# A graph network on one core: TensorE transposes for the first graph's input and for the tiles of the last five graphs

## The chip, the core and the metric

One Trainium2 core runs the whole program: 64 graphs, one after the other through the same layers. The time is the device time of one execution in microseconds, the median of three runs. The core has a matrix engine (TensorE, PE in the profile), a vector engine (VectorE, DVE), an activation engine (ScalarE, ACT), GpSimd (POOL) and a queue that issues transfers (SyncE, SP). They run side by side and wait for one another through semaphores; each takes its own instructions in the order in which the program lists them.

## What is computed

Every graph has 256 nodes with 256 features (float32) and an adjacency matrix of 256 x 256 integers. Four layers follow one another, each with a residual and a layer norm:

```python
x: (64, 256, 256)   adj: (64, 256, 256)
# layer 0: attention over 8 heads of 32 under the mask adj | adj.T | eye, then a feed-forward of 1024
qkv = x @ Wqkv.T + bqkv
x = norm(x + norm(norm(x + softmax(mask(q k^T / sqrt(32))) v @ Wo.T + bo) + relu(. @ W1.T + b1) @ W2.T + b2))
# layers 1 and 2: graph attention ("gat")
h = x @ W;  e = leaky_relu(f_i + g_j) under the mask;  x = norm(x + softmax(e) @ h [+ bias, or elu])
# layer 3: two relational convolutions ("conv"), rel is adj == 1
h = elu(x @ w_root + b + (rel^T @ x / deg) @ w_rel)   # twice
x = norm(x + h)
```

TensorE contracts over the partition axis, of which there are 128. A product `x @ W` therefore needs x with the features on the partitions, that is, transposed. Each graph needs this six times: for the input of the attention, for the feed-forward, for the two gats and for the two convs.

## The kernel before

The kernel first writes down all operations of all graphs with an engine, an assumed cost, and the tiles that they read and write. A list scheduler then sorts them by due times; what it puts out is the fixed order of instructions on each engine. The due times of the last five graphs lie close together (`LAST, SPACE = 5, 0.1`), so that these graphs run interleaved at the end.

```python
RINGS = {"x": 3, "adj": 4, ..., "T": 4, ..., "blocks": 1, "turned": 1, "xT": 2}   # buffers of each kind
LAG = {"PE": 0.21, "DVE": 0.13, "ACT": 0.13, "POOL": 0.08, "SP": 4.5}
PERIOD = 46.0
LAST, SPACE = 5, 0.1
```

There are three ways of transposing. The first is that of the feed-forward: four TensorE transposes into one PSUM bank, and a copy by ScalarE.

```python
def transposed(xt):
    xT, pt = new("T", [P, KB, N]), new("bank", [P, KB, N])
    def issue():
        for kb in range(KB):
            for i in range(NB):
                nc.tensor.transpose(pt()[:, kb, i * P : (i + 1) * P], xt()[:, i, kb * P : (kb + 1) * P], ident)
    pe("full", 0.44, issue, [xt], [pt], [xT])
    act(0.47, lambda: nc.scalar.copy(xT(), pt()), [pt], [xT])
    return xT
```

The second, the "bounce", serves the gats and the convs. VectorE transposes each 32 x 32 block within the tile; four transfers write the blocks to device memory in the right places, and one reads the whole back. The rows come back in another order of the features (feature 32 b + c at partition 4 c + b), so the weights of these layers are loaded in that order too (`spread` in the setup).

```python
def bounced(xt):
    turned, rows, xT = new("turned", ...), new("rows", ...), new("T", [P, NB * KB, P])
    dve(0.63, lambda: nc.vector.transpose(turned().rearrange("p b q n -> p (b q n)"),
                                          xt().rearrange("p i (k c b) -> p b (i k) c", k=KB, b=4)), [xt], [turned], "uses")
    for a in range(4):
        op("SP", 0.5, lambda a=a: nc.sync.dma_start(rows()..., turned()[32 * a : 32 * a + 32]...), ...)
    op("SP", 0.5, lambda: nc.sync.dma_start(xT()..., rows()...), [rows], [xT], lag=BACK)
    return xT, lambda kb, i: xT()[:, KB * i + kb, :]
```

The third serves the input. Eight loads bring the blocks of x to their places straight from the input, 32 floats at a time, and VectorE transposes the blocks.

```python
def input_transposed():
    blocks, xT = new("blocks", [P, KB, N // 32, 32]), new("xT", [P, KB, N])
    for a in range(4):
        for kb in range(KB):
            f = kb * P + 32 * a
            op("SP", 0.51, lambda ...: nc.sync.dma_start(blocks()[32 * a : 32 * a + 32, kb],
               x_in[g, :, f : f + 32].rearrange("(m r) c -> r m c", r=32)), [], [(blocks, 4 * kb + a)])
    dve(0.62, lambda: nc.vector.transpose(xT()..., blocks()...), [blocks], [xT], "uses")
    return xT
```

The setup and one graph, cut:

```python
def setup():
    load(c_wqkv, wqkv, "WqkvT")          # one transfer of 768 KB
    load(c_wo, wo, "WoT"); load(c_w1, w1, "W1T"); load(c_w2, w2, "W2T")
    ...                                  # gat and conv weights

def projections(xT):                     # q and k in halves, then v
    ...  pe("full", 0.86, product(wqkv[:, kb, n * P : (n + 1) * P], xT...), [xT, c_wqkv], [pq], [qk])
    ...  pe("full", 0.86, product(xT..., wqkv[:, kb, 2 * D : 3 * D]),       [xT, c_wqkv], [pv], [v])

# one graph
xT = input_transposed()
adj = load("adj", adj_graph[g], I32)
am, gm = masks(adj)
xt = load("x", x_graph[g], F32)
add_row_later(xt, bo, [c_bo])
ctxT = attention(xT, am)
x1 = product_plus(...); layer_norm(x1)
xt = feed_forward(x1, load("xr", x_graph[g], F32))
xt = layer1(xt, gm)                      # gat: begins with bounced(xt)
xt = layer2(xt, gm)                      # gat
rel = relation(load("adj", adj_graph[g], I32))
h = conv(conv(xt, 0, rel, rdeg), 1, rel, rdeg)   # each begins with bounced(.)
add(h, xt); layer_norm(h)
op("SP", 0.4, lambda: nc.sync.dma_start(out_graph[g], h()), [h], [])
```

Of the kernel before, what the change touches and what calls it, by code (L numbers as in the profile page):

```python
# [8 lines left out]
F32 = mybir.dt.float32  # L9
# [8 lines left out]
P = 128  # L18
# [2 lines left out]
BIG = 1e30  # L21
NO_EDGE = -346.0


SENT, BACK = 3.0, 4.5

# [186 lines left out]
def tile_gnn_stack(ctx: ExitStack, tc: tile.TileContext, t: dict, out: bass.AP):  # L213
# [16 lines left out]
    nc = tc.nc  # L230
    x_in, adj_in = t["x"], t["adj"]
    B, N, D = x_in.shape
# [253 lines left out]
    def main_path(plan):  # L486
# [19 lines left out]
        def setup():  # L506


            def load(w, to, name, rel=None):
                view = t[name] if rel is None else t[name][rel]  # L510
                n = view.shape[0] * view.shape[1] / (256 * 256)
                plan.op("SP", 0.85 * n, lambda: nc.sync.dma_start(to, view.rearrange("(c p) n -> p c n", p=P)), 0, [], [w])

            def spread(w, to, name, rel=None):

                view = (t[name] if rel is None else t[name][rel]).rearrange("(k b c) n -> b c k n", b=4, c=32)
                for b in range(4):
                    plan.op("SP", 0.6, lambda b=b: nc.sync.dma_start(to[b::4], view[b]), 0, [], [w])

            load(c_wqkv, wqkv, "WqkvT")  # L520
            load(c_wo, wo, "WoT")
            load(c_w1, w1, "W1T")
            load(c_w2, w2, "W2T")
            for i, names in enumerate((("L1_WT", "L1_W"), ("L2_W", "L2_WT"))):

                wt = plan.tile("T", [P, KB, D], F32)
                plan.op("SP", 0.85, lambda wt=wt, n=names[1]: nc.sync.dma_start(wt(), t[n].rearrange("(c p) n -> p c n", p=P)),
                        0, [], [wt])
                spread(c_gw[i], gw[i][:, :, 0:D], names[0])
                for kb in range(KB):  # L530
                    pa = plan.tile("bank", [P, 2], F32)

                    def issue(i=i, kb=kb, wt=wt, pa=pa):
                        for c in range(KB):
                            nc.tensor.matmul(pa(), lhsT=wt()[:, c, kb * P : (kb + 1) * P], rhs=av[i][:, :, c],
                                             start=(c == 0), stop=(c == KB - 1))

                    plan.op("PE", 0.9, issue, 0, [wt], [pa], mode="full")
                    plan.op("DVE", 0.2, lambda i=i, kb=kb, pa=pa: nc.vector.tensor_copy(ga[i][:, kb, :], pa()),
                            0, [pa], [c_ga[i]])  # L540
                for b in range(4):
                    plan.op("SP", 0.6, lambda i=i, b=b: nc.sync.dma_start(gw[i][b::4, :, D : D + 2], ga[i][32 * b : 32 * b + 32]),
                            0, [c_ga[i]], [c_gw[i]])
            for i in range(2):
                spread(c_cw[i], conv_w[i][:, :, 0:D], f"w_root{i + 1}")
                spread(c_cw[i], conv_w[i][:, :, D:], f"w_rel{i + 1}", 1)


            pb = plan.tile("bank", [P, D], F32)

            def bias_out():
                for c in range(KB):
                    nc.tensor.matmul(pb(), lhsT=bqkv[:, 2 * KB + c : 2 * KB + c + 1].to_broadcast([P, P]), rhs=wo[:, c, :],
                                     start=(c == 0), stop=(c == KB - 1))

            plan.op("PE", 0.9, bias_out, 0, [c_wo], [pb], mode="full")
            plan.op("DVE", 0.34, lambda: nc.vector.tensor_tensor(bo, pb(), bo, op=ALU.add), 0, [pb], [c_bo])


            pf = plan.tile("bank", [P, NF], F32)  # L560
            for f in range(NF):
                def shift(f=f):
                    for c in range(KB):
                        nc.tensor.matmul(pf()[:, f : f + 1], lhsT=w1[:, c, f * P : (f + 1) * P], rhs=bcol[:, c : c + 1],
                                         start=(c == 0), stop=(c == KB - 1))

                plan.op("PE", 0.9, shift, 0, [c_w1], [pf], mode="full")
            plan.op("DVE", 0.2, lambda: nc.vector.tensor_tensor(b1, pf(), b1, op=ALU.add), 0, [pf], [c_b1])
            for c in range(KB):
                plan.op("DVE", 0.7, lambda c=c: nc.vector.tensor_scalar(w1[:, c, :], w1[:, c, :], gcol[:, c : c + 1], None,  # L570
                                                                        op0=ALU.mult), 0, [c_w1], [c_w1])

        def graph(g):
# [9 lines left out]
            def act(cost, issue, reads, writes):  # L583
                op("ACT", cost, issue, reads, writes)
# [4 lines left out]
            def tok(ring, dtype=F32):  # L589
                return new(ring, [P, NB, D], dtype)  # L590

            def load(ring, view, dtype):
                xt = tok(ring, dtype)
                op("SP", 0.85, lambda: nc.sync.dma_start(xt(), view), [], [xt])
                return xt
# [15 lines left out]
            def transposed(xt):  # L611
# [9 lines left out]
                act(0.47, lambda: nc.scalar.copy(xT(), pt()), [pt], [xT])  # L621
                return xT

            def bounced(xt):

                turned, rows, xT = new("turned", [P, 4, NB * KB, 32]), new("rows", [P, NB * KB, 4, 32]), new("T", [P, NB * KB, P])
                dve(0.63, lambda: nc.vector.transpose(turned().rearrange("p b q n -> p (b q n)"),  # L629
                                                      xt().rearrange("p i (k b c) -> p b (i k) c", k=KB, b=4)),  # L630
                    [xt], [turned], "uses")
                for a in range(4):
                    op("SP", 0.5, lambda a=a: nc.sync.dma_start(  # L633
                        rows().rearrange("(c b) q a n -> c (b q) a n", b=4)[:, :, a, :],
                        turned()[32 * a : 32 * a + 32].rearrange("c b q n -> c (b q) n")), [turned], [(rows, a)], lag=SENT)
                op("SP", 0.5, lambda: nc.sync.dma_start(xT().rearrange("p q n -> p (q n)"), rows().rearrange("p q a n -> p (q a n)")),
                   [rows], [xT], lag=BACK)
                return xT, lambda kb, i: xT()[:, KB * i + kb, :]
# [70 lines left out]
            def projections(xT):  # L709

                qk, v = new("qk", [P, 2 * KB, N]), tok("v")
                for half in range(2):
                    pq = new("bank", [P, KB, N])
                    for c in range(KB):
                        n = half * KB + c
                        pe("full", 0.86, lambda n=n, c=c, pq=pq: product(
                            pq()[:, c, :], lambda kb: wqkv[:, kb, n * P : (n + 1) * P], lambda kb: xT()[:, kb, :], KB),
                           [xT, c_wqkv], [pq], [qk])
                    for c in range(KB):
                        n = half * KB + c  # L720
                        if half == 0:
                            act(0.36, lambda n=n, c=c, pq=pq: nc.scalar.activation(
                                qk()[:, n, :], pq()[:, c, :], AF.Identity, bias=bq[:, c : c + 1], scale=scale), [pq], [(qk, n)])
                        else:
                            act(0.36, lambda n=n, c=c, pq=pq: nc.scalar.activation(
                                qk()[:, n, :], pq()[:, c, :], AF.Identity, bias=bqkv[:, n : n + 1]), [pq], [(qk, n)])
                pv = new("bank", [P, NB, D])
                for i in range(NB):
                    pe("full", 0.86, lambda i=i: product(pv()[:, i, :], lambda kb: xT()[:, kb, i * P : (i + 1) * P],
                                                         lambda kb: wqkv[:, kb, 2 * D : 3 * D], KB), [xT, c_wqkv],  # L730
                       [pv], [v])
                act(0.47, lambda: nc.scalar.copy(v(), pv()), [pv], [v])
                return qk, v
# [83 lines left out]
                return y  # L817

            def gat(xt, layer, gm, seen, bias, finish):
                xT, xT_at = bounced(xt)  # L820
                w, c_w = gw[layer], c_gw[layer]
                h, e, z = new("h", [P, NB, HW]), tok("e"), tok("X")
                for i in range(NB):
# [70 lines left out]
            def conv(h, layer, rel, rdeg):  # L894
# [1 line left out]


                w, c_w, bias = conv_w[layer], c_cw[layer], conv_b[layer]
                hT, hT_at = bounced(h)
                o, hi, lo, n = tok("o"), new("hi", [P, NB, D + 2], F32R), tok("lo", F32R), tok("e")  # L900
                cols = D if layer else D + 2
                for i in range(NB):
# [33 lines left out]
                    [n, o], [o], "uses")  # L936
                return o

            xT = input_transposed()
            adj = load("adj", adj_graph[g], I32)  # L940
            am, gm = masks(adj)
            xt = load("x", x_graph[g], F32)
            add_row_later(xt, bo, [c_bo])
            ctxT = attention(xT, am)
            x1 = product_plus(lambda c: ctxT()[:, c, :], [ctxT, c_wo], lambda c: wo[:, c, :], KB, xt)
# [277 lines left out]
```

## Time and profile before

| | us |
|---|---|
| median of three runs | 2896.01 |
| the three runs | 2893.25 to 2898.55 |
| span of the profiled execution | 2897.1 |
| TensorE busy | 2805.3 (97%) |
| VectorE busy | 2523.0 (87%) |
| ScalarE busy | 1540.4 (53%) |
| GpSimd busy | 789.1 (27%) |

The profile page gives, for one execution, the busy time of each engine, the span in 40 equal slices (each digit is the busy share in tenths), the chain of waits that ended last, and groups of like instructions. A group's line names the line of the kernel, the engine, the operation, what it writes and reads with shapes, how many there are, and after the bar the busy time and the mean length in ns; after the second bar stands the engine's idle time just before them, and what ended it. Line 657 is the helper that issues all products, line 618 the TensorE transposes, line 629 the VectorE transpose of the bounce, line 633 its writes to device memory and line 636 the read back. Line 650 is the VectorE transpose of the input. A float32 product has two records in the trace for each instruction.

### The profile page before, as it was taken

The page shows a single profiled execution, that of the slowest core. Times are in us where ns is not written, and L with a number is a line of the kernel's source. Part 1 is how long each engine was busy: PE and PEld are TensorE (multiplying, and loading weights), DVE is VectorE, ACT ScalarE, POOL GpSimd, SP SyncE. Part 2 cuts the span into 40 slices and gives each one's busy share as a digit, 9 for nine tenths or more (in the row PEclk, how much of TensorE's full clock was granted, in tenths as well). Part 3 has the DMA queues.
Part 4 walks back from the last instruction along what each step waited for, and adds up shares of the span by engine and source line. Part 5 has one row for each costly group of instructions (what it writes and reads, how often), then busy time and mean ns, then how long its engine had stood idle before and what let it go on. Part 6 is the DMA issues. An engine that isn't in the chain of part 4 may idle for free.

```text
span 2897.1 us, 50588 instructions
## 1 busy us (share of the span) xinstructions
PE 2805.3 (97%) x16182; PEld 2128.1 (73%) x16182; DVE 2523.0 (87%) x6557; ACT 1540.4 (53%) x3713; POOL 789.1 (27%) x1685
## 2 busy tenths in 40 slices
PE   8999999999999999999999999999999999999975
PEld 6776777777777767777777777777777777777853
DVE  6879899989989898999889898899888998999686
ACT  3555555546455555655555465555555655555343
POOL 2232223222223222222222322232231332222221
PEclk9999999999999999999999999999999999999998
DMA  7454455445444444454444544444444544443342
GB/s 183 81 108 88 99 101 102 89 101 102 95 92 100 87 94 94 98 101 93 104 97 93 98 99 99 100 91 102 86 93 96 109 88 93 105 90 72 67 83 70
DMA packets 844512, 278.32 MB, mean 96 GB/s; under 512 B 692656, under 2 KB 810672, under 8 KB 844240
## 3 DMA queue, kind: packets, MB, share of 16 engines
q1 hardware_dynamic: 808800, 240.27, 37.7%
q0 software_dynamic: 35440, 34.76, 8.5%
q8 instruction: 131, 2.15, 0.3%
q14 instruction: 141, 1.16, 0.1%
HBM read 157.43 MB, written 83.89 MB: 83 GB/s over the span
## 4 chain that ended last, share of the span: by engine, by line
PE 82%; DVE 10%; ACT 3%; DMA 2%; issue 2%; POOL 1%; SPq 1%; DVEq 0%; POOLq 0%; ACTq 0%
PE bank L657 67%; PE bank L919 4%; PE bank L776 3%; PE bank L751 3%; PE bank L771 2%; DMA rows<-turned 2%; DVE p L759 1%; PE bank L618 1%; DVE turned L629 1%; PE bank L839 1%; SPq L633 1%; DVE st L666 1%; DVE o L929 1%; DVE both L763 1%; DVE e L844 1%
## 5 line engine op out<-in xcount | busy, mean ns | idle before, releaser
L671 POOL TENSOR_SCALAR rstd<-mv 128x2 f32<-128x2 f32 x384 | 104.4, 272 | 1869.8 <-DVE mv L668 1496.7
L678 ACT ACTIVATE X<-X,rstd 128x256 f32<-128x256 f32 x640 | 349.8, 597 | 244.7 <-POOL rstd L674 230.1
L657 PE MATMUL bank<-cw,T 128*128 128x512 f32 x1024 | 467.9, 600 | 9.6 <-DMA T<-rows 9.1
L657 PE MATMUL bank<-T,w 128*128 128x256 f32 x2048 | 471.6, 380 | 5.2 <-ACT p L757 2.6
L657 PE MATMUL bank<-w,hid 128*128 128x256 f32 x2048 | 460.1, 380 | 0.0
L657 PEld LDWEIGHTS bank<-w,hid 128*128 128x128 f32 x2048 | 385.9, 190 | 62.7 <-issue 10.4
L657 PEld LDWEIGHTS bank<-T,w 128*128 128x128 f32 x2048 | 382.7, 190 | 64.5 <-issue 6.9
L757 ACT ACTIVATE p<-bank 128x512 f32<-128x512 f32 x512 | 299.9, 598 | 87.8 <-PE bank L751 87.6
L657 PEld LDWEIGHTS bank<-cw,T 128*128 128x128 f32 x1024 | 192.2, 192 | 209.3 <-issue 195.2
L759 DVE TENSOR_TENSOR p<-p,am 128x512 f32<-128x512 f32 x512 | 332.8, 680 | 10.8 <-ACT p L757 10.7
L672 POOL TENSOR_TENSOR rstd<-rstd,neghalf 128x2 f32<-128x2 f32 x384 | 305.7, 796 | 32.1
L809 ACT ACTIVATE hid<-bank,col_b 128x256 f32<-128x256 f32 x512 | 209.4, 474 | 113.8 <-PE bank L657 112.1
L657 PE MATMUL bank<-xT,wqkv 128*128 128x256 f32 x1024 | 251.6, 387 | 13.4 <-DVE xT L650 12.9
L657 PE MATMUL bank<-h,e 128*128 128x259 f32 x1024 | 253.8, 388 | 11.0 <-ACT e L849 9.3
L657 PE MATMUL bank<-gw,T 128*128 128x258 f32 x1024 | 249.1, 384 | 2.1 <-ACT inv L783 1.5
L657 PEld LDWEIGHTS bank<-h,e 128*128 128x128 f32 x1024 | 192.7, 192 | 66.6 <-issue 19.3
L666 DVE BATCH_NORM_STATS2 st<-X 128x6 f32<-128x256 f32 x640 | 237.5, 413 | 1.8
L906 ACT CAST hi<-bank 128x256 fp32r<-128x256 f32 x256 | 94.6, 370 | 263.4 <-PE bank L657 262.6
L657 PEld LDWEIGHTS bank<-xT,wqkv 128*128 128x128 f32 x1024 | 189.7, 192 | 54.0 <-issue 13.5
L780 DVE RECIPROCAL inv<-bank 128x256 f32<-128x256 f32 x128 | 220.0, 1734 | 8.8 <-PE bank L776 8.6
L657 PEld LDWEIGHTS bank<-gw,T 128*128 128x128 f32 x1024 | 191.1, 191 | 36.7 <-issue 5.2
L629 DVE STREAM_TRANSPOSE turned<-X 128x512 f32<-128x512 f32 x192 | 134.9, 703 | 45.0 <-DMA rows<-turned 23.0
(121 smaller groups left out, 4775.4 us busy)
## 6 DMA issues: line engine op xcount, KB each, us to landing
rows<-turned SPq DMA_DIRECT2D x1024, 64.0 KB, 2.2
T<-rows SPq DMA_DIRECT2D x256, 256.0 KB, 2.8
adj<-in_adj_dram SPq DMA_DIRECT2D x128, 256.0 KB, 3.0
blocks<-in_x_dram SPq DMA_DIRECT2D x512, 32.0 KB, 2.3
x<-in_x_dram SPq DMA_DIRECT2D x64, 256.0 KB, 3.0
xr<-in_x_dram SPq DMA_DIRECT2D x64, 256.0 KB, 2.8
xr<-row_ln_b POOLq DMA_DIRECT2D x64, 256.0 KB, 4.4
x<-row_bo POOLq DMA_DIRECT2D x64, 256.0 KB, 4.8
```

Source lines behind the costliest of these rows:

```text
L629: dve(0.63, lambda: nc.vector.transpose(turned().rearrange("p b q n -> p (b q n)"), xt().rearrange("p i (k b c) -> p b (i k) c", k=KB, b=4 ...
L657: nc.tensor.matmul(dst, lhsT=lhs(c), rhs=rhs(c), start=(c == 0), stop=(c == n - 1))
L666: nc.vector.bn_stats(stat()[:, i, :], y()[:, i, :])
L671: nc.gpsimd.tensor_scalar(rstd()[:, 0, :], mv()[:, :, 1], 1.0, EPS, op0=ALU.mult, op1=ALU.add)
L672: nc.gpsimd.tensor_tensor(rstd()[:, 0, :], rstd()[:, 0, :], neghalf[:, 0:NB], op=ALU.pow)
L678: nc.scalar.activation(y()[:, i, :], y()[:, i, :], AF.Identity, bias=rstd()[:, 1, i : i + 1], scale=rstd()[:, 0, i : i + 1])
L757: act(0.58, lambda pr=pr, k=k, sr=s[r]: nc.scalar.activation(pr(), sr(), AF.Exp, accum_out=seen_sum[:, k : k + 1]), [s[r]], [pr])
L759: dve(0.60, lambda pr=pr, kt=kt: nc.vector.tensor_tensor(pr(), pr(), am()[:, kt, None, :].to_broadcast([P, KB, N]), op=ALU.mult), [pr, am] ...
L780: dve(1.62, lambda hg=hg, pc=pc: nc.vector.reciprocal(inv()[:, hg, :], pc()[:, 1, :]), [pc], [(inv, hg)])
L809: act(0.36, lambda f=f, k=k, ph=ph: nc.scalar.activation(hid()[:, f + k, :], ph()[:, k, :], AF.Relu, bias=b1[:, f + k : f + k + 1]), [ph, ...
L906: act(0.27, lambda i=i, po=po: nc.scalar.copy(hi()[:, i, 0:D], po()[:, D:]), [po], [(hi, i)])
L919: nc.tensor.matmul(pa()[:, 0:n], lhsT=rel()[:, i, j * P : (j + 1) * P], rhs=part()[:, i, 0:n], start=(c == 0), stop=(c == len(terms) - 1))
```

## The change

It has three parts. Graph 0 no longer loads its input in blocks: the plain load of x, which the residual needs anyway, is issued first, and TensorE transposes it. Wqkv is loaded in three transfers of 256 KB, one each for q, k and v, so that a product waits only for its own part. And the last five graphs (`QUICK = 5`) no longer bounce their tiles through device memory in the gats and convs: ScalarE rearranges the features into the order that the weights expect, TensorE transposes the tile, and ScalarE copies it out of PSUM. The first two are meant to let the first product start earlier; the third is meant to shorten the chain of each of the last graphs, when no later graph is left to fill the waits.

```diff
+QUICK = 5
...
-            load(c_wqkv, wqkv, "WqkvT")
+            for n in range(3):
+                plan.op("SP", 0.85, lambda n=n: nc.sync.dma_start(
+                    wqkv[:, :, n * D : (n + 1) * D], t["WqkvT"].rearrange("(c p) n -> p c n", p=P)[:, :, n * D : (n + 1) * D]),
+                    0, [], [(c_wqkv, n)])
...
+            def rearranged(xt):
+                if g < B - QUICK:
+                    return bounced(xt)
+                spread = tok("turned")
+                act(0.8, lambda: nc.scalar.copy(spread().rearrange("p i (k c b) -> p (i k) c b", k=KB, b=4),
+                                                xt().rearrange("p i (k b c) -> p (i k) c b", k=KB, b=4)), [xt], [spread])
+                xT = transposed(spread)
+                return xT, lambda kb, i: xT()[:, kb, i * P : (i + 1) * P]
...
-                           [xT, c_wqkv], [pq], [qk])
+                           [xT, (c_wqkv, half)], [pq], [qk])
...
-                                                         lambda kb: wqkv[:, kb, 2 * D : 3 * D], KB), [xT, c_wqkv],
+                                                         lambda kb: wqkv[:, kb, 2 * D : 3 * D], KB), [xT, (c_wqkv, 2)],
...
             def gat(xt, layer, gm, seen, bias, finish):
-                xT, xT_at = bounced(xt)
+                xT, xT_at = rearranged(xt)
...
-                hT, hT_at = bounced(h)                # in conv
+                hT, hT_at = rearranged(h)
...
-            xT = input_transposed()
+            if g == 0:
+                xt = load("x", x_graph[g], F32)
+                xT = transposed(xt)
+            else:
+                xT = input_transposed()
             adj = load("adj", adj_graph[g], I32)
             am, gm = masks(adj)
-            xt = load("x", x_graph[g], F32)
+            if g > 0:
+                xt = load("x", x_graph[g], F32)
```

The scheduler runs anew on the changed list. It lists the same operations for graphs 1 to 58, but their order on the engines differs from the sixth graph on.

## The prediction

> **What bounds the kernel now.** I read the page's slices first, then stretches of 100 us, then the first and the last piece of the chain of waits, then the groups by line and shape.
>
> ```profile
> PE   8999999999999999999999999999999999999975
> DVE  6879899989989898999889898899888998999686
> ```
> TensorE is over 90% busy in all slices but the first and the last two.
>
> The stretches give the size of these two ends (columns: length, busy us of PE, weight loads, VectorE, ScalarE, GpSimd with counts, granted clock, DMA share, GB/s):
>
> ```profile
> 0.00:100.00 100.00, 85.99 (x574) 69.41 (x578) 64.03 (x133) 38.52 (x101) 26.40 (x48) 0.95 0.67 155
> ...
> 2600.00:2700.00 100.00, 100.00 (x617) 76.67 (x617) 91.28 (x211) 56.03 (x138) 25.54 (x59) 1.00 0.35 74
> 2700.00:2800.00 100.00, 86.65 (x372) 69.54 (x371) 68.95 (x215) 40.10 (x85) 26.44 (x66) 0.95 0.38 74
> 2800.00:2900.00 100.00, 62.46 (x203) 33.67 (x201) 64.70 (x196) 35.05 (x70) 12.67 (x36) 0.87 0.33 73
> ```
> The page's 2805.3 us of PE in a span of 2897.1 leave 91.8 us idle: 14 in the first 100 us, some 30 strewn over the middle, 48 after 2740 us. There the clock also falls, to 0.95 and 0.87. The change aims at both ends; in the middle an engine is full that it does not relieve.
>
> The start, in the chain of waits (start, length, what):
>
> ```profile
> 0.74 5.22 DMA wqkv<-in_WqkvT_dram
> 5.96 0.02 issue
> 5.98 6.08 DMA blocks<-in_x_dram
> 12.06 0.02 issue
> 12.09 0.72 DVE xT L650
> 12.81 0.04 issue
> 12.85 5.64 PE bank L657 x16
> ```
> The first matmul waits for eight small loads and the VectorE transpose behind them; the weights had been there since 5.96.
>
> The last of the trips through device memory, same view:
>
> ```profile
> 2870.06 0.62 DVE turned L629
> 2870.68 0.32 DVE lo L907
> 2871.00 0.26 SPq L633
> 2871.30 0.64 SPq L633
> 2871.98 0.63 SPq L633
> 2872.65 2.21 DMA rows<-turned
> 2875.00 2.59 DMA T<-rows
> 2877.73 5.09 PE bank L657 x8
> ```
> From the VectorE transpose to the first product is 7.67 us, and the eight matmul records after it took 5.09 us, where the same eight at 2866.20 took 3.59.
>
> The prices of what is added, from the groups:
>
> ```profile
> L629 DVE STREAM_TRANSPOSE turned<-X 128x512 f32<-128x512 f32 x192 | 134.9, 703 | 45.0 <-DMA rows<-turned 23.0 <-ACT X L678 21.0 <-issue 0.2
> L849 ACT ACTIVATE e<-e 128x512 f32<-128x512 f32 x128 | 80.8, 631 | 113.6 <-DVE e L847 107.3 <-DVE h L832 3.4 <-DVE r L854 2.5
> L618 PE MATMUL bank<-ident,X 128*128 128x128 f32 x256 | 39.9, 277 | 2.7 <-ACT X L678 1.9 <-ACT p L757 0.8
> L621 ACT COPY T<-bank 128x512 f32<-128x512 f32 x64 | 37.5, 588 | 40.7 <-PE bank L618 40.3
> ```
>
> **What the Trainium skill says.** "VectorE: DVE Perf Modes", section "The three transpose paths": VectorE turns only 32x32 blocks, TensorE a full 128x128 into PSUM. The kernel agrees: its VectorE transpose needs the trip through memory to bring the blocks to their places. "DMA: Bandwidth & Descriptors", section "Anatomy of one DMA — SWDGE (gpsimd) path": a DMA has a fixed cost of about 2.0 us, mostly the receipt of the last write. It speaks of the other queue, but the trace agrees in size: 2.2 us for the 64 KB writes, 2.8 us for the 256 KB read back, and a bounce pays both in turn. "TensorE: Matmul & The Clock Gate", section "HAM oscillation — how this bites in real kernels": gaps of some microseconds let the clock fall back. The 5.09 against 3.59 us agrees. "SBUF — State Buffer", section "Door 1: The DMA port swizzle": accesses that cross to a new 16-byte line pay. The new ScalarE rearrangement reads every 32nd float; no run here shows its cost yet.
>
> **The change part by part.**
>
> Head. The eight loads (issued from 1.24 to 6.3 us) and the 0.72 us transpose go for graph 0. One load of x, 256 KB in 1 KB rows, is issued first; its median landing in the run is 3.0 us, so about 0.74 + 3.3 = 4.0 us. Four TensorE transposes: the chain shows 0.44 us for four at full clock, so 0.9 cold. ScalarE's copy 0.59, hand-overs 0.3 together: the product may start at 5.9. The first two parts of Wqkv with x are 768 KB, what Wqkv alone was before, and that landed at 5.96. I put the first product at 6.3 us instead of 12.85, a gain of 6.5. The table load of ScalarE (1.28 us) waits for nothing in the new order, so it is over before. As TensorE works through one dependent chain until about 39 us, the gain should pass on; the loads of W1, Wo, W2 and graph 1 must come earlier too, with the DMA 0.74 to 1.02 busy up to 40 us. I take off 0.5: **6 us**.
>
> Tail. The last matmul of the last feed-forward ends at 2741.5, so the tail is 2897.1 - 2741.5 = 155.6 us. The instruction order puts behind that matmul 48 products of 512 columns, 82 of 258 or 259, 96 of the gather and 20 spreads (a product has two records). At full-clock rates of the trace (3.60 us for four; 17.32 us for forty of 256 columns; about 1.0 for eight of the gather; 0.22 for two spreads) that is 43.2 + 35.5 + 12 + 2.2 = 93 us of TensorE. The very end, from the last 512-column product to the finish, is 2897.1 - 2877.7 = 19.4 us, 17.9 at full clock, and holds 4.6 us of that work. So a perfect tail would be 93 - 4.6 + 17.9 = 106; 49 us are lost.
>
> New in the tail: 19 of the 20 bounces lie there by the order (76 transposes), 19 x 0.44 = 8.4 us of TensorE, and two gat products more, 0.9. The perfect tail becomes 115. VectorE loses 19 x 0.70 = 13.4 us of 114 (sum of the 20 us stretches from 2740 on), ScalarE gets 19 x (0.8 + 0.59) = 26 on top of 59. The 0.8 is an estimate: 0.63 for a 128x512 pass from and to SBUF, plus something for the stride. Neither becomes the bound.
>
> Latency: a bounce goes from 7.67 us to about 0.8 + 0.44 + 0.59 and three hand-overs of 0.15 = 2.3, so 5.4 us less. For the last graph the two conv bounces lie where TensorE has little else: 2 x 5.4 = 10.8, plus 2 x 1.5 for products that no longer start at a lower clock. The two gat bounces are mostly covered by four other graphs' work, and more TensorE work stands against them: 5 or so more, of which the 9 us of new TensorE work takes part. I let the lost 49 us fall to about 24: 115 + 24 = 139 us, a gain of **17 us** (from 5 to 28).
>
> The buffer helps too: "turned" is a single one. Before, a bounce holds it 0.7 + 2.6 + 2.2 = 5.5 us (transpose, four issues, landing), 19 times in 155.6 us, two thirds of the tail; after, some 1.6 us.
>
> Middle. Nothing is added, but the scheduler's order differs on TensorE from row 875 of 9646 on, about the sixth graph. The 30 us of scattered idle there fall otherwise: plus or minus 6 us, mean zero.
>
> Sum: 2896.0 - 6 - 17 = **2873 us**.
>
> **The rivals.**
>
> 1. The tail is bound by VectorE, not by latency. For it: VectorE is 0.9 busy between 2740 and 2760 and 114 of 155.6 us in the tail, and its adds and casts head many waits (products waiting for hi 7.5 and for lo 5.9 us). Then the gain is little more than the 13 us of VectorE taken away, with ScalarE copies in its place in the chain: 5 to 10 us, 2880 to 2885. Against it: VectorE does 91 to 99 of 100 in the middle while TensorE stays full.
> 2. The tail becomes nearly full, since five graphs with short chains cover one another: loss 10 us, tail 125, gain 30; 2860. Against it: the old tail lost 49 us though it also had five graphs to choose from, and LayerNorm on GpSimd and the exponentials stay in each chain.
> 3. The head's gain is swallowed: weights or graph 1's blocks arrive no sooner and TensorE waits at 25 to 39 us. For it: DMA share near 1 up to 20 us. Against it: the small packets of eight loads are gone, and graph 1's blocks need no buffer of graph 0 any more. It would cost up to 5 of the 6 us.
> 4. The shuffled middle costs more than the ends gain: one stretch, 1000 to 1100 us, idles 5.9 us already; several such would make 2890 or so.
>
> **Range and chances.** The tail's spread (5 to 28) is the largest term, then the middle's 6, then the head's 2: together some 12 us either way for 8 in 10, widened a little as the order of a whole program is new: 2858 to 2888. Two per cent are 58 us; that is more than all idle at the two ends could give with the new TensorE work counted in, so faster by over 2% gets 0.02. Slower by over 2% would need 58 us of new stalls in a middle that idles 30: 0.01. The rest, 0.97, within 2%.
>
> **What would show it.** Head: the first 256-column product at 6 to 7 us; the second graph's product (39.2 before) near 33. Tail: from the last feed-forward product to the end 130 to 150 us; no DMA of rows in the chain there; the rearrangement 0.7 to 1.0 us each; the clock after 2740 above the 0.87 of before. TensorE idle in the middle between 24 and 36 us. Wrong would be: a rearrangement of over 1.2 us, a chain in the tail made of VectorE alone, or a head that stalls on a weight.

## The result, and the profile after

| | before | after |
|---|---|---|
| median, us | 2897.01 | 2875.05 |
| range of four runs, us | 2893.25 to 2898.55 | 2872.27 to 2875.57 |
| ratio, 95% interval | | 0.9924 [0.9907, 0.9941] |
| span of the profiled execution, us | 2897.1 | 2872.8 |

The change takes 22 us, 0.76%. (The excerpt of `bounced` further up shows one pattern as `(k c b)`; in the kernel it is `p i (k b c) -> p b (i k) c`.)

Busy tenths of the changed kernel, in 40 slices of the span:

```profile
PE   8999999999999999999999999999999999999987
DVE  6879889888889888997988988997989989889677
```
For TensorE only the last two slices differ, 8 and 7 for 7 and 5. The same stretches as before, for the changed kernel:

```profile
0.00:100.00 100.00, 91.64 (x596) 73.11 (x597) 66.53 (x141) 41.91 (x110) 28.48 (x52) 0.93 0.66 155
...
2600.00:2700.00 100.00, 100.00 (x618) 76.75 (x616) 90.48 (x213) 56.54 (x138) 25.54 (x57) 1.00 0.32 69
2700.00:2800.00 100.00, 89.96 (x413) 72.85 (x412) 65.45 (x219) 54.50 (x104) 25.33 (x66) 0.97 0.11 22
2800.00:2872.80 72.80, 54.92 (x217) 33.12 (x215) 52.08 (x169) 45.36 (x84) 11.61 (x32) 0.91 0.11 31
```
TensorE idles 5.7 us less in the first 100 us (91.64 against 85.99 busy). At the end ScalarE takes over what the DMA engines did: 54.50 us busy for 40.10, DMA share 0.11 for 0.38.

For everything that follows I cut an execution in three: the head up to the first product of the second graph, the middle up to the last matmul of the last feed-forward, and the tail. From the two profiles:

| us | head | middle | tail | PE idle in the tail |
|---|---|---|---|---|
| before | 39.62 | 2701.9 | 155.6 | 48.0 |
| after | 36.66 | 2699.1 | 137.0 | 27.9 |
| gain | 3.0 | 2.8 | 18.6 | 20.1 |

**The head.** TensorE's timeline, before (start, length, line, what, how many records, in brackets the idle time ahead and what ended it):

```profile
12.85 5.64 PE L657 MATMUL bank<-xT,wqkv 128*128 128x256 f32 x16 [12.85 <-DVE xT L650]
...
23.88 3.18 PE L564 MATMUL bank<-col_ln_b,w 128*128 128x1 f32 x28
27.97 2.35 PE L771 MATMUL bank<-both,ones 128*32 128x256 f32 x7 [0.91 <-DVE both L763]
...
34.43 1.95 PE L535 MATMUL bank<-a,T 128*128 128x2 f32 x16
36.63 3.20 PE L657 MATMUL bank<-wo,ctxT 128*128 128x256 f32 x8 [0.25 <-DVE ctxT L781]
39.62 0.63 PE L657 MATMUL bank<-xT,wqkv 128*128 128x256 f32 x1
```
and after (with one line of VectorE, for ctxT):

```profile
3.64 1.09 PE L623 MATMUL bank<-ident,x 128*128 128x128 f32 x4 [3.64 <-DMA x<-in_x_dram]
5.40 6.10 PE L672 MATMUL bank<-T,wqkv 128*128 128x256 f32 x16 [0.68 <-ACT T L626]
...
19.03 5.08 PE L569 MATMUL bank<-col_ln_b,w 128*128 128x1 f32 x28
24.04 1.08 PE L786 MATMUL bank<-both,ones 128*32 128x256 f32 x8
...
28.11 1.05 PE L540 MATMUL bank<-a,T 128*128 128x2 f32 x8
30.18 0.69 DVE L796 TENSOR_TENSOR ctxT<-bank,inv 128x256 f32<-128x256 f32 x2
31.41 1.84 PE L540 MATMUL bank<-a,T 128*128 128x2 f32 x8 [2.25 <-DMA T<-in_L_WT_dram]
33.11 3.76 PE L672 MATMUL bank<-wo,ctxT 128*128 128x256 f32 x8
36.66 3.60 PE L672 MATMUL bank<-xT,wqkv 128*128 128x256 f32 x15
```
Read down the starts: the changed kernel is 7.45 us ahead at the first product, 3.9 at the sums over the heads (`both,ones`), 3.5 at the product with Wo and 3.0 at the second graph. So 4.5 us are lost on the way.

The end of this stretch can be read in full. ctxT, which the Wo product multiplies, is ready at 30.87 (30.18 + 0.69); before, it released that product at 36.63. Up to here some 5.7 us of the lead are left. But in TensorE's order the products with a weight of the gat (`a,T`) stand ahead of the Wo product, and TensorE waits 2.25 us for that weight. The Wo product therefore starts 2.2 us after ctxT is ready, where it followed at once before. It then takes 0.6 us more itself (3.55 for 2.99 us until the next product).

The other 1.7 us went earlier. The same 28 small products take 5.08 us for 3.18, at a lower clock (the records grant 0.66 between 20 and 40 us, and 0.76 before), and hold up the sums behind them. But from the sums to the first `a,T` product it is 4.07 us, and 6.46 before, so most of this delay is won back, and the 1.9 us must not be added to the wait.

SyncE's queue says why the gat's weight is late:

```profile
17.28 9.60 SPq L662 DMA_DIRECT2D blocks<-in_x_dram  x8
26.92 0.50 SPq L532 DMA_DIRECT2D T<-in_L_WT_dram  x1
```
Its load is issued behind the eight block loads of the second graph, whose issue takes 9.60 us, over a microsecond each.

The head is not the same in every profile. In the ten kernels of this document that load Wqkv in three parts, the changed one included, the wait for this weight is 0 to 4.84 us. In all nine others TensorE also waits, 0.17 to 1.95 us, for the next part of Wqkv; the longest, with ten graphs:

```profile
9.41 5.49 PE L672 MATMUL bank<-T,wqkv 128*128 128x256 f32 x12 [1.95 <-DMA wqkv<-in_WqkvT_dram]
```
The first product starts early in each of them (5.34 to 5.45), but what comes behind it meets weights that are not there yet.

**The tail.** The last trip between VectorE's result and the product, after (where 7.67 us stood before):

```profile
2850.08 1.14 ACT L634 COPY turned<-o 128x512 f32<-128x512 f32 x1 [0.65 <-DVE o L950]
...
2851.27 0.66 PE L623 MATMUL bank<-ident,turned 128*128 128x128 f32 x4
2851.47 1.09 ACT L693 ACTIVATE o<-o,rstd 128x256 f32<-128x256 f32 x2 [0.25 <-POOL rstd L689]
2852.47 0.56 ACT L626 COPY T<-bank 128x512 f32<-128x512 f32 x1
...
2853.08 5.37 PE L672 MATMUL bank<-cw,T 128*128 128x512 f32 x8 [1.15 <-ACT T L626]
```
3.00 us. Two things are not as predicted: the rearrangement takes 1.14, and the copy out of PSUM starts 0.5 us late, because another graph's layer norm (L693) stands ahead of it on ScalarE. The groups, by shape (busy us, mean ns of one; then idle before, and its causes):

```profile
L634 ACT COPY turned<-X 128x512 f32<-128x512 f32 x15 | 16.5, 1101 | 4.4 <-PE bank L623 2.5 <-DMA rows<-turned 1.9
L623 PE MATMUL bank<-ident,turned 128*128 128x128 f32 x80 | 12.8, 284 | 6.5 <-ACT turned L634 6.5
L634 ACT COPY turned<-o 128x512 f32<-128x512 f32 x5 | 5.5, 1100 | 1.4 <-DVE o L950 1.4
```
What TensorE waited for in the tail (us in total, times, longest), before:

```profile
PE bank L657 <- DMA T<-rows: 9.4, 3, 5.7
PE bank L919 <- DVE hi L912: 7.5, 5, 2.4
PE bank L657 <- ACT e L849: 7.4, 5, 2.2
PE bank L919 <- DVE lo L907: 5.9, 8, 1.7
```
and after:

```profile
PE bank L623 <- ACT turned L634: 6.5, 5, 3.6
PE bank L672 <- ACT T L626: 3.9, 5, 1.2
PE bank L934 <- DVE hi L927: 1.8, 2, 1.1
PE bank L934 <- DVE lo L922: 1.7, 2, 1.2
PE bank L672 <- ACT e L864: 0.8, 1, 0.8
```
The wait for the returning rows is gone; the largest that took its place is the new one, for the rearrangement. Added up, TensorE's waits for the transposed tile itself are no shorter: 9.4 us before, 6.5 + 3.9 after. The 20.1 us come off the other waits, above all those for hi and lo (13.4 to 3.5), two conversions that the change does not touch, and for e (7.4 to 0.8), the exponentials of the gat. Two of the experiments below, the added VectorE work and the second buffer, bear on why.

### The profile page after: what moved, and what is told of

It reads as the page before. It is cut to its first block, busy times and chain, and to the rows that moved or that the text cites. A ratio compares the mean times of both kernels' runs of the same rounds, so it can differ in the third digit from the quotient of the medians.

```text
span 2872.8 us, 50523 instructions
## 1 busy us (share of the span) xinstructions
PE 2808.4 (98%) x16266; PEld 2136.0 (74%) x16266; DVE 2510.5 (87%) x6536; ACT 1569.0 (55%) x3754; POOL 790.9 (28%) x1685
## 3 DMA queue, kind: packets, MB, share of 16 engines
q14 instruction: 139, 1.14, 0.1%
## 4 chain that ended last, share of the span: by engine, by line
PE 82%; DVE 9%; ACT 2%; DMA 2%; SPq 2%; issue 2%; POOL 1%; DVEq 0%; POOLq 0%; ACTq 0%
PE bank L672 68%; PE bank L934 4%; PE bank L791 3%; PE bank L766 3%; PE bank L786 2%; DMA rows<-turned 1%; PE bank L623 1%; PE bank L854 1%; DVE p L774 1%; DVE inv L795 1%; DVE st L681 1%; DVE turned L644 1%; DMA T<-in_L_W_dram 1%; ACT X L693 1%; ACT p L772 1%
## 5 line engine op out<-in xcount | busy, mean ns | idle before, releaser
L693 ACT ACTIVATE X<-X,rstd 128x256 f32<-128x256 f32 x640 | 349.5, 596 | 231.2 <-POOL rstd L689 209.0
L672 PE MATMUL bank<-xT,wqkv 128*128 128x256 f32 x1008 | 244.4, 384 | 0.1
L672 PEld LDWEIGHTS bank<-gw,T 128*128 128x128 f32 x1024 | 191.9, 191 | 43.2 <-issue 7.8
L778 DVE TENSOR_TENSOR both<-p 128x512 f32<-128x512 f32 x256 | 166.4, 680 | 0.0
```

Source lines behind the costliest of these rows:

```text
L672: nc.tensor.matmul(dst, lhsT=lhs(c), rhs=rhs(c), start=(c == 0), stop=(c == n - 1))
L693: nc.scalar.activation(y()[:, i, :], y()[:, i, :], AF.Identity, bias=rstd()[:, 1, i : i + 1], scale=rstd()[:, 0, i : i + 1])
L778: dve(0.60, lambda r=r: nc.vector.tensor_tensor(both[r](), p[0, r](), p[1, r](), op=ALU.add), [p[0, r], p[1, r]], [both[r]], "uses")
```

## The experiments

Every kernel's profile, cut as above (one execution each; the medians and ratios below come from several).

| us | head | middle | tail | PE idle in the tail |
|---|---|---|---|---|
| before | 39.62 | 2701.9 | 155.6 | 48.0 |
| after | 36.66 | 2699.1 | 137.0 | 27.9 |
| head only | 36.06 | 2701.1 | 150.5 | 48.2 |
| tail only | 40.01 | 2706.3 | 137.2 | 28.5 |
| period 46.5 | 37.49 | 2717.7 | 134.3 | 26.6 |
| other ScalarE lag | 40.95 | 2721.7 | 136.7 | 28.1 |
| a VectorE transpose more | 37.56 | 2702.8 | 134.6 | 27.9 |
| two buffers, old path | 40.93 | 2704.2 | 144.4 | 38.9 |
| last graph only | 38.0 | 2702.6 | 137.8 | 35.6 |
| ten graphs | 35.28 | 2708.9 | 129.7 | 23.1 |
| Wqkv whole | 39.74 | 2714.1 | 135.1 | 28.7 |
| first two graphs | 35.67 | 2699.8 | 134.4 | 28.2 |
| weights in natural order | 38.14 | 2702.7 | 122.9 | 20.6 |
| natural order, first two graphs | 34.02 | 2697.9 | 123.4 | 21.1 |

**Head alone and tail alone.** The changed kernel with

```diff
-QUICK = 5
+QUICK = 0
```

> Only the head of the change: graph 0's input by TensorE and Wqkv in three parts; the last five graphs bounce as before. Theory: the first product starts at 5.4 us, but the second graph's first product only about 3 us earlier than before (39.6), since TensorE meets a weight load (T for layer 2) and a cold clock on the way; the time falls by 3 us plus or minus 6 for the new order of the middle, 2894; the tail stays near 155 us. Rival, the whole 7.5 us of the head arrive at the end: second graph's first product at 32 us, time 2889.

Measured: 2895.78 us against 2899.76, ratio 0.9985 [0.9977, 0.9992], so 4.0 us (2.3 to 6.7 by the interval). And the changed kernel with the head of before:

```diff
-            if g == 0:
-                xt = load("x", x_graph[g], F32)
-                xT = transposed(xt)
-            else:
-                xT = input_transposed()
+            xT = input_transposed()
...
-            for n in range(3): ...           # Wqkv in three loads
+            load(c_wqkv, wqkv, "WqkvT")
```

> Only the tail of the change: the last five graphs by TensorE; head as before. Theory: the tail (last feed-forward product to end) falls from 155.6 to 137 us, plus or minus 4, and the time to 2878 plus or minus 6. Rival, the gain of the whole change was luck of the new order in the middle: the tail stays above 148 us.

Measured: 2882.19 us against 2899.76, ratio 0.9938 [0.9925, 0.9952], 17.6 us (13.9 to 21.7). The two add up to 21.6 of the 22.0 us of the whole. So close a sum is in part chance: the intervals are wider, and each of these kernels has an order of its own in the middle. Head-only's profiled execution was 6 us under that kernel's median, so for the head's worth I take the median.

**Other orders of the same operations.** The scheduler is given another period, or a lag of ScalarE that differs in the third decimal; the operations are those of the changed kernel.

```diff
-    PERIOD = 46.0
+    PERIOD = 46.5
```

> The changed kernel with the scheduler's PERIOD at 46.5 instead of 46.0: the same operations in another order. Theory: the middle moves by at most 6 us either way, the tail stays within 4 us of 137; time 2869 to 2881. Rival, the order decides: the time moves by 10 us or more, or the tail by 8.

Measured: 2889.57 us, 0.9965 [0.9952, 0.9979]. That is 14.5 us over the changed kernel, so the rival holds: the middle is 18.6 us longer, the tail is not (134.3).

```diff
-    LAG = {"PE": 0.21, "DVE": 0.13, "ACT": 0.13, "POOL": 0.08, "SP": 4.5}
+    LAG = {"PE": 0.21, "DVE": 0.13, "ACT": 0.131, "POOL": 0.08, "SP": 4.5}
```

> The changed kernel with one assumed lag of the scheduler at 0.131 instead of 0.130, which gives another order of the same operations without any intent. Theory, the middle (graph 1's first product to the last feed-forward) lies within 8 us of the 2699 of the change, and the tail within 4 of 137: time 2867 to 2885. Rival, the order of the changed kernel is a lucky one: the middle is longer by 10 us or more, as in the run with the other period (2718).

Measured: 2899.22 us, 1.0005 [0.9996, 1.0013]: the whole gain is gone. The table says where: the tail is still 136.7, the middle 22.6 us longer than in the changed kernel. Sums of five stretches of 500 us from 100 to 2600 us, changed kernel:

```profile
sum 2500.00, PE 2471.87 PEld 1880.16 DVE 2235.97 ACT 1370.72 POOL 699.95; mean PE 494.37 PEld 376.03 DVE 447.19 ACT 274.14 POOL 139.99
```
and with the other lag:

```profile
sum 2500.00, PE 2460.33 PEld 1867.12 DVE 2218.68 ACT 1362.11 POOL 703.55; mean PE 492.07 PEld 373.42 DVE 443.74 ACT 272.42 POOL 140.71
```
TensorE idles 2471.87 - 2460.33 = 11.5 us more there. No single wait carries it; the largest of TensorE's in this kernel between 100 and 2700 us is

```profile
PE bank L672 <- ACT T L626: 6.9, 9, 1.3
```
The other half of the 22.6 us is time in which TensorE counts as busy. The groups of the middle show where the largest part of it lies, first in the changed kernel, then with the other lag:

```profile
L786 PE MATMUL bank<-both,ones 128*32 128x256 f32 x1008 | 84.5, 385 | 2.0 <-DVE both L778 2.0
L786 PE MATMUL bank<-both,ones 128*32 128x256 f32 x1008 | 91.6, 385 | 4.4 <-DVE both L778 4.2
```
The sums over the heads fill 7.1 us more, though a record is no longer: 1008 records of 385 ns are 388 us in both, so on average 4.6 of them run side by side in the one and 4.2 in the other. (Groups overlap, so 7.1 us is not the exact share.) Why this order parts them was not tried, nor were other orders of the kernel before.

**Is VectorE the bound of the tail?** One more 128x512 VectorE transpose, into a buffer of its own that nobody reads, for each of the 20 tiles of the last five graphs:

```diff
+                more = new("more", [P, NB * D])
+                dve(0.63, lambda: nc.vector.transpose(more(), xt().rearrange("p i n -> p (i n)")), [xt], [more], "uses")
                 spread = tok("turned")
```

> The changed kernel, and each of the 20 tiles is passed once more through VectorE (a transpose of 0.70 us into a buffer that nobody reads). Theory, the tail is a mix of chains and VectorE is not the bound by itself: the tail grows by 3 to 7 us, time 2878 to 2882. Rival, VectorE bounds the tail: it grows by the full 13 us (19 of 0.70), time 2888. If latency alone counts: under 2 us.

Measured: 2876.92 us, 0.9918 [0.9905, 0.9932]. The tail of the changed kernel (columns as in the stretches above):

```profile
2735.84:2872.80 136.96, 109.05 (x458) 74.51 (x456) 102.90 (x343) 86.40 (x160) 27.88 (x78) 0.93 0.10 24
```
and of this one:

```profile
2740.30:2874.90 134.60, 106.72 (x459) 72.92 (x457) 111.80 (x359) 86.45 (x160) 27.25 (x79) 0.95 0.10 25
```
Of the 20 added transposes 16 lie in the tail. VectorE has 8.9 us more, nearly its 114.1 us of before the change, and the tail is no longer; TensorE's idle time stays at 27.9 us. So VectorE is not the bound, and the work taken from it does not explain the gain.

**The single buffer.** The kernel before, with two buffers for turned blocks:

```diff
-         ... "blocks": 1, "turned": 1, "xT": 2}
+         ... "blocks": 1, "turned": 2, "xT": 2}
```

> The kernel before with two buffers instead of one for the tile that waits for its writes to device memory; nothing else. Theory, the length of a bounce made the old tail long, not the single buffer: the tail falls by less than 5 us from 150 to 156. Rival, the single buffer serialised the bounces: the tail falls by 10 us or more and comes near the 137 of the change.

Measured: 2893.42 us against 2899.01, 0.9983 [0.9976, 0.9990]. The tail falls from 155.6 to 144.4, and the head and the middle give 3.6 of that back. The old path's tail varies by itself: head-only's is 150.5 with the same idle time of TensorE (48.2 us), but busy for 102.3 us at a granted clock of 0.94, where before had 107.6 us at 0.89. This run's clock is 0.89 too, so the 11.2 us against before are the fairer figure. Idle time falls by 9.1 us, nearly half of the 20.1 of the change. TensorE's waits in this tail:

```profile
PE bank L657 <- DMA T<-rows: 12.7, 5, 4.2
PE bank L919 <- DVE hi L912: 2.1, 2, 1.4
PE bank L919 <- DVE lo L907: 1.4, 2, 0.7
```
Those for hi and lo are down to 3.5 us, as in the changed kernel, though VectorE is still busy for 112.1 us. So the rival is nearer than the theory: the old path was slow to a good part because tiles queued for one buffer. The changed kernel's tail is still 7 us shorter than this one's, with 11 us less idle time, which fits its shorter trip.

**How many graphs?** Only the last graph, then ten:

```diff
-QUICK = 5
+QUICK = 1
```

> Only the last graph transposes its gat and conv tiles on TensorE; the four before it bounce through memory. If the tail's gain is the last graph's own chain, whose conv bounces nothing covers, most of it stays: tail (last feed-forward product to the end) 140 to 144 us. If it needs all five graphs freed of the single buffer for turned blocks, the tail lies near 150. My own theory shares it between the two: about 146 us. The head is as in the changed kernel (first product 5.4 us, second graph's at 36 to 38 us). The whole: 2875 to 2890 us, as the middle falls anew.

Measured: 2880.09 us against 2898.38, 0.9937 [0.9921, 0.9954]. Its tail:

```profile
2740.63:2878.40 137.77, 102.13 (x394) 65.44 (x393) 109.29 (x353) 64.27 (x128) 26.86 (x76) 0.92 0.31 68
```
137.8 us, under all that was expected: the last graph alone brings the tail to within 0.8 us of five graphs'. With five, TensorE is busy 109.05 - 102.13 = 6.9 us more (the tail has 15 more sets of four transposes, 6.6 us at 0.44) and idle 7.7 us less. The other four graphs earn what they cost. Of the 5.6 us between the two profiles 4.8 lie in the head and the middle.

```diff
-QUICK = 5
+QUICK = 10
```

> Ten graphs instead of five transpose on TensorE. The theory that the change pays only where TensorE has gaps: the 20 more sets of four transposes lie where it is full and add 20 x 0.44 = 9 us, so 2884 us, with the tail (last feed-forward product to the end) unchanged at 134 to 137 us and TensorE busy 9 us more. The rival, that the bounces also cost TensorE waits in the full stretch: the added work is paid back by fewer waits, 2875 us or less, and idle time in the middle (28 us) falls by several us.

Measured: 2874.73 us, 0.9917 [0.9900, 0.9933]. Neither theory stands alone. The middle is 9.8 us longer, about the added 9 us, and its idle time is the same (28.4 us for 28.3), which speaks for the first; but other orders alone have moved the middle by more than this. The tail is 7.3 us shorter and the head 1.4, which neither foresaw. Three more sets of transposes lie in this tail than with five graphs; whether they account for it was not tried.

**Wqkv in one load**, all else as changed:

```diff
-            for n in range(3): ...           # Wqkv in three loads
+            load(c_wqkv, wqkv, "WqkvT")
```

> Wqkv is loaded in one transfer, all else as in the changed kernel. If the three parts matter: with x in front the whole weight lands about 1 us later than its first part, so the first product starts at 6.3 to 7 us instead of 5.4, and the wait for Wo stays. If they don't: 5.4 to 5.8 us. Either way the second graph's product stays at 36 to 38 us and the time is within the spread of the middle's orders, 2865 to 2890 us.

Measured: 2888.13 us against 2898.38, 0.9966 [0.9953, 0.9978]. TensorE's timeline:

```profile
5.90 1.09 PE L620 MATMUL bank<-ident,x 128*128 128x128 f32 x4 [5.90 <-DMA x<-in_x_dram]
9.94 0.58 PE L707 MATMUL bank<-ident_b,bits 128*128 128x128 bf16 x4 [2.96 <-DVE ident_b L329]
10.32 2.02 PE L669 MATMUL bank<-T,wqkv 128*128 128x256 f32 x4
```
The first product starts at 10.32, far beyond the expected 7. The scheduler now issues the big load first, x lands at 5.90 instead of 3.64, and it puts the mask's transposes ahead of the product, which wait for a constant until 9.94. The head ends at 39.74, as before the change: in the order that comes out without the split, transposing the first input on TensorE gains nothing. Between the two profiles this kernel is 16.1 us behind the changed one, 3.1 in the head and 15.0 in the middle, less 1.9 in the tail.

**The second graph's input by TensorE too**, so that no block loads stand in SyncE's queue early:

```diff
-            if g == 0:
+            if g < 2:
```

> The changed kernel, with graph 1's input also loaded plainly and transposed by TensorE, so that its eight block loads no longer stand before the weights on the transfer queue. Theory, the head lost 4.5 of its 7.5 us to the late load of T for layer 2: the output product of graph 0 starts at or before 31 us instead of 33.1 and graph 1's first product at 34 or before instead of 36.7; the time falls by 2 to 3 us, within the plus or minus 8 of a new order in the middle. Rival, the cold clock of TensorE alone: graph 1's product stays at 36 us or later.

Measured: 2873.11 us against 2899.01, 0.9915 [0.9901, 0.9929]. The gat's weight is issued at 24.20 instead of 26.92 and TensorE no longer waits for it, but the second graph starts at 35.67, only 1 us earlier and later than expected. The Wo product waits for ctxT instead, which comes 3 us later in this profile than in the changed kernel's:

```profile
33.84 1.99 PE L672 MATMUL bank<-wo,ctxT 128*128 128x256 f32 x8 [0.35 <-DVE ctxT L796]
```
Kernels with the changed kernel's head start the second graph anywhere from 35.28 to 38.14 (and at 40.95 with the lag of 0.131, where the wait for the gat's weight is 4.84 us), so 1 us here says little.

**Without the rearrangement.** The gat and conv weights are loaded a second time in the natural order of the features, the conv weights into buffers that the attention no longer uses, and the last graphs take TensorE's transpose straight from the tile:

```diff
-                spread = tok("turned")
-                act(0.8, lambda: nc.scalar.copy(spread()..., xt()...), [xt], [spread])
-                xT = transposed(spread)
+                xT = transposed(xt)
...                                      # second loads of the weights, later listing of the convs
```

> The changed kernel without ScalarE's rearrangement: for the last five graphs the weights of the gats and convs are loaded a second time in the natural order of the features, and TensorE transposes the tile itself. Theory, what is left of the tail is chains: each bounce loses 1.1 us of ScalarE and a hand-over, four in the last graph, so the tail falls from 137 to about 132 (128 to 134). Rival, TensorE and VectorE are full by now: the tail stays within 2 us of 135 to 137.

Measured: 2863.13 us (2861.18 to 2865.52), 0.9873 [0.9858, 0.9889]. Its tail:

```profile
2740.91:2863.80 122.89, 102.28 (x454) 70.89 (x453) 101.82 (x342) 67.61 (x138) 28.50 (x76) 0.96 0.08 23
```
14 us less than the changed kernel's 136.96, more than expected. ScalarE does 18.8 us less. Of the 14 us, 7.3 are idle time of TensorE (20.6 for 27.9). The other 6.8 are nearly all shorter matmuls, at a granted clock of 0.96 for 0.93: the 96 records of 512 columns take 43.2 us for 44.8, and others follow. (One set of four transposes fewer lies in this tail.) It is not the rearrangement alone. The conv parts of the last five graphs are also listed later than in the changed kernel, and the tiles no longer pass through the single buffer `turned`, for which the rearrangement stood waiting for 4.4 us (2.5 for the transposes that read it, 1.9 for a bounce's writes). The changed kernel with a second such buffer was not tried.

**Both**, the last one with the second graph's input by TensorE:

> The version without the ScalarE rearrangement, and graph 1's input transposed by TensorE too. The earlier run of this head change moved the second graph's product by 1 us. So: second graph's product about 36 to 37 us, tail 120 to 125 us as without it, and about 2862 us (2855 to 2870, as the middle falls anew). If the blocks of graph 1 held the first graph's weights back: second graph's product at 34 us or less and 2859 us.

Measured: 2857.97 us (2857.02 to 2864.40) against 2898.38, ratio 0.9867 [0.9851, 0.9884]. It beats the changed kernel (0.9924 [0.9907, 0.9941]); from the version without the second graph's part the intervals don't tell it apart. The second graph starts at 34.02, at the edge of what the second theory named, with no wait for a gat weight.

## Why the prediction came out right

The time was 2875 for a predicted 2873, and both end terms point the right way: the tail's gain is real and near its predicted size. That the sum came so close is in part luck. Several terms were mis-sized and partly cancel, and of three orders of the same operations two, 2889.6 and 2899.2, lie outside the predicted 2858 to 2888.

1. **First product: predicted at 6.3, measured 5.40.** x came at 3.64, not 4.0; transposes, hand-overs and copy took 1.76, not 1.9. The table load of ScalarE was over, as said.
2. **The head's gain "should pass on": predicted 6 us, 3.0 in the profile and 4.0 (2.3 to 6.7) by head-only's median.** This is the step that failed. I took off 0.5 us for crowding; of the 7.45 us at the first product 4.5 were gone at the second graph: 2.2 in the wait for a gat weight ahead of the Wo product, 0.6 in that product and 1.7 before it. "A head that stalls on a weight" was one of the prediction's own signs of being wrong, and it came true. Rival 3 named the right kind of wait; what I held against it, that the second graph's blocks need no buffer of the first any more, is beside the point, as it is their place in the queue that delays the weight. Taking them away took the wait away, but not surely more time than the scatter of heads.
3. **Wqkv in parts.** It was put down as a part of the first product's time, without a figure of its own; without it, and in the order that then comes out, the head gains nothing (39.74).
4. **Tail: predicted 17 us, 18.6 in the profile, 17.6 by tail-only's median.** The added TensorE work (8.4 us for 19 bounces) fits the 6.9 us for 15, a difference of two tails in which other groups move too. The prediction gave 13.8 of the gain to the last graph and little net to the other four: the last gave 12.7 to 17.8 (by which old tail one takes), the four 0.8. The mechanism is half confirmed. The prediction put the gain down to the length of the last graph's trips, and with that graph alone changed the tail falls as far; but that also frees the shared buffer, and summed over the tail TensorE's waits for transposed tiles did not shrink (9.4 to 10.4 us), while those for hi, lo and e did. No run separates the shorter trip from the free buffer in full.
5. **Bounce: predicted 2.3 us, measured 3.00.** The rearrangement was put at 0.8 (0.7 to 1.0): 1.10. One copy also stood behind a layer norm. The term "2 x 1.5 for products at a lower clock" held for one of two at most: the last product still takes 5.37 us (5.09 before) after an idle time of only 1.15 us.
6. **"The buffer helps too"** had no figure, and was the term most underrated: two buffers alone take 6 to 11 us off the tail, and 9.1 of the 20.1 us of idle time.
7. **Middle: predicted zero, plus or minus 6; measured -2.8**, inside, but the width was wrong. Fourteen kernels, most with an order of their own, gave middles from 2697.9 to 2721.7, most of them longer than before's 2701.9. The argument from 30 us of scattered idle time looked at the idle time of one order only. Rival 4 did not come true here, and did with a lag changed by 0.001.
8. **Rival 1** (VectorE) falls by the added transposes. **Rival 2** (a tail of 125) was not reached with the rearrangement in the path, and was without it.
9. **Two readings** were off, without weight for the sum: the second graph's product started at 39.62 before, not 39.2, and VectorE is busy for 84 to 95 us of each 100 in the middle, not 91 to 99.

## What to carry to other kernels

Where a pipeline drains, shorten the chain of the last item first: one of five graphs brought nearly the whole gain in the tail. Ask first whether the items only queue for a buffer: here a second one, a change of one digit, gave nearly half of the idle time back. A faster path that needs a reordering pass may do better with the order moved into data that are loaded once, here the weights; the run that did so was 12 us faster, though it changed more than that. And where a scheduler fixes the order of a long program, measure a few orders of the unchanged operations before believing a gain below one per cent: here they spread as far as the gain itself.

## What the runs showed of the hardware

- A ScalarE copy of 128x512 floats that reads every 32nd float takes 1.10 us, where passes of the same size without the stride take 0.63. The Trainium skill, "SBUF — State Buffer", section "Door 1: The DMA port swizzle", says that each access that crosses to a new 16-byte line pays a penalty and gives no figure for ScalarE. The direction agrees: 0.47 us more here for 512 elements a partition. That the lines are the cause was not tried.
- VectorE's transpose of the bounce reads the tile in a permuted order too, and takes 0.70 us whether it permutes (701 ns) or reads straight through (701 ns for the added ones). It moves runs of 32 neighbouring floats, so this is no test of reading every 32nd float.
- The Trainium skill, "TensorE: Matmul & The Clock Gate", section "HAM oscillation — how this bites in real kernels", ties the fall of the clock to gaps of some microseconds. Before, a gap of 5.71 us preceded the 5.09 us product; after, the gap just before it was 1.15 us and the product took 5.37. A short gap straight ahead is then no sign of full speed; what set the clock here was not tried.
